# Attention sums of four batches kept in one bank per key head, and new values of four batches added together

## The chip, the core and the metric

The kernel runs on one core of a Trainium2 chip. Time is the device time of one execution in microseconds (us). Before the change the median of three runs was 2500.81 us (2497.43 to 2500.87).

The engines are named as in the profile: PE is the tensor engine (PEld its weight loads), DVE the vector engine, ACT the scalar engine, POOL the GpSimd engine, SP the engine that only issues DMA transfers. DMA transfers run on queues of their own. The tensor engine writes only to PSUM, a memory of eight banks, each of 512 float32 values in each of 128 partitions; the other data lie in SBUF.

## The reference

Four residual layers follow each other. Only the third, attention over a paged cache, is touched by the change.

```python
x = x + _L0_cond_ref(x, cond, w0)            # a 32x32 mix per batch
x = x + _L1_cond_ref(x, adapter, ...)        # linear layer and LoRA
x = x + _L2_cond_ref(x, Wq, Wk, Wv, Wo, ...) # attention
x = x + _L3_cond_ref(x, cond, w3)            # a 32x32 mix per batch

# _L2_cond_ref: 64 batches of 32 tokens, 32 query heads, 8 key heads, head size 128
q, k, v = x @ Wq.T, x @ Wk.T, x @ Wv.T       # then rms norm and rotary on q and k
kc = k_cache[block_table]                    # 16 pages of 32 keys per batch
vc = v_cache[block_table]
k_all = concatenate([kc, k], axis=1)         # 512 cached keys and 32 new ones
v_all = concatenate([vc, v], axis=1)
scores = einsum('bqhd,bkhd->bhqk', q, k_all) * SCALE
scores = where(valid, scores, -1e30)
o = einsum('bhqk,bkhd->bqhd', softmax(scores), v_all)
return o.reshape(bsz, seqlen, HQ * D) @ Wo.T
```

## The kernel before

The 2048 rows (64 batches of 32 tokens) make 16 tiles of 128 rows, that is of NB = 4 batches. The 8 key heads make NG = 2 groups of KG = 4. A step is one group and one tile, 32 in all; in the text below "a tile" of the attention is such a step. A step has four units, one for each batch, and a unit has four slots, one for each key head k of its group. So a step has 16 slots and the attention 512. A key head serves REP = 4 query heads, and 4 heads of 32 tokens give the 128 rows of one matmul.

The slots are a software pipeline written by hand. `slot(i)` (L1193) emits, in this order, what belongs to slot i: the scores of slot i (L838 and L841, two matmuls into the two banks of `s_ps`), the `flip` of slot i - 2 (L880: its probabilities are transposed, four blocks into the one bank of `pT_ps`, which VectorE copies to `pT`), pieces of the projection of later tiles (L651), and the `values` of slot i - 3 (L893: four matmuls over the cached values `v_sb`). Each engine executes what it is given in that order. Other work is put into slots by a plan, `at(slot, where, ...)`, and `run(i, where)` emits it at its place in the slot: "fetch" first, "act" and "store" last.

Three pieces of other work matter here.

New values. The 32 new keys of a unit have values too. The probabilities of the four key heads for them are transposed together (`flip_new`, L873) into `pT_new`, and `values_new` (L905) adds four matmuls with 32 rows each, one for each key head, at the end of each unit: 128 times.

Heads and pages. The projected queries and keys are normed and rotated by DVE, and four heads at a time are transposed on PE (`Norm.turn`, L756) and copied by ACT (`Norm.keep`, L768). During the first group's steps the key pages of the second group are turned likewise (`Turn.turn`, L272, and `Turn.keep`, L283).

Sums, copies and stores. Four banks of PSUM belong to the sums: three under the tag `o` for the key heads 0 to 2, and one, tag `o3`, for key head 3, which the heads and pages that are turned use as well. At the end of each unit `finish` copies the four sums to `oT` by two ACT copies (L919 and L922). At the end of a step, one slot later, `store` writes the whole `oT` (1 MB) to memory as one DMA (L929), on SP's queue, or on POOL's for the last three steps. The last layer reads it back later.

SP issues most transfers in order. In the "fetch" of every fourth slot it loads the keys of the next unit page by page: 16 DMAs (L794) into one of two buffers, after register loads from the page table. `fetch_new` (L816) loads `v_new`. `begin` (L825) puts a unit's new keys beside the cached ones. The cached values are gathered by POOL (L105).

The tile pools name their buffers: a tile with the same name goes round through `bufs` buffers, 2 by default in the pool `attn`, 1 in the PSUM pools. A new use waits until the last reader of that buffer is done, a DMA included.

Of the kernel before, what the change touches and what calls it, by code (L numbers as in the profile page):

```python
# [27 lines left out]
F32 = mybir.dt.float32  # L28
# [15 lines left out]
P = 128  # L44
B, S, HID = 64, 32, 512
NT = B * S // P
NB = P // S
NC = HID // P
D = 128
HK, REP = 8, 4  # L50
NPAIR = HK // 2
NG = 2
KG = HK // NG
# [24 lines left out]
def resid_kernel(  # L78
# [19 lines left out]
    nc = tc.nc  # L98
# [129 lines left out]
    with ExitStack() as l2:  # L228
# [11 lines left out]
        room = {}  # L240
# [8 lines left out]
        class Turn:  # L249
# [15 lines left out]

            def turn(self):
                if self.g:
                    self.ps = room["o"].tile([P, HID], F32, name="pageT_ps", tag="o3")
                else:
                    self.ps = ps_s.tile([P, 2 * HID], F32, name="s_ps")  # L270
                for k in range(KG):
                    nc.tensor.transpose(  # L272
                        self.ps[:, k * P : (k + 1) * P],
                        self.rows[:, k // 2, (k % 2) * D : (k % 2 + 1) * D],
                        ident,
                    )
# [10 lines left out]
            def store(self):  # L287
                c = self.c
                nc.sync.dma_start(
                    out=v_dram[self.g][c * P : (c + 1) * P, :].rearrange("k (i f) -> k i f", i=2),  # L290
                    in_=self.cached(1),
                )
                nc.sync.dma_start(
                    out=kT_dram[self.g][4 * c : 4 * c + 4].rearrange("p d f -> d p f"),
                    in_=self.turned.rearrange("d p k s -> d p (k s)"),
                )
# [400 lines left out]
        class Norm:  # L697
# [50 lines left out]
                nc.vector.tensor_tensor(self.a, self.a, self.b, ALU.add)  # L748

            def turn(self):  # L750
                if "o" in room:
                    self.tp = room["o"].tile([P, REP, P], F32, name="head_ps", tag="o3")
                else:
                    self.tp = ps_t.tile([P, REP, P], F32, name="head_ps", tag="t")
                for h in range(REP):
                    nc.tensor.transpose(self.tp[:, h, :], self.a[:, h, :], ident)  # L756

# [15 lines left out]
        class Unit:  # L773
# [38 lines left out]

            def fetch_new(self):

                self.v_new = room["v"].tile([P, D], F32, name="v_new", bufs=2)
                nc.sync.dma_start(  # L816
                    out=self.v_new,
                    in_=vn_dram[self.g][self.t][self.j * S : (self.j + 1) * S, :].rearrange(
                        "s (k d) -> k s d", k=KG
                    ),  # L820
                )

            def begin(self):

                nc.scalar.copy(  # L825
                    self.kT[:, NPP].rearrange("p k s -> p (k s)"),
                    step_of[self.s].kT_new[:, self.j].rearrange("p k s -> p (k s)"),
                )
                self.new = room["attn"].tile([P, KG, S], F32, name="p_new")
                self.sm, self.total, self.pT, self.o_ps = {}, {}, {}, {}  # L830

            def scores(self, k):

# [32 lines left out]
            def flip_new(self):  # L866


                if last_scores:
                    ps = last_scores.pop()[:, :P]  # L870
                else:
                    ps = ps_s.tile([P, 2 * HID], F32, name="s_ps")[:, :P]
                nc.tensor.transpose(ps, self.new.rearrange("p k s -> p (k s)"), ident)  # L873
                self.pT_new = room["attn"].tile([P, P], F32, name="pT_new", bufs=1)
                nc.scalar.copy(self.pT_new, ps)

            def flip(self, k):
# [6 lines left out]
            def values(self, k):  # L884


                if k == 0:
                    self.o_three = room["o"].tile([P, KG - 1, HID], F32, name="o_ps", tag="o")
                    self.o_ps = {i: self.o_three[:, i, :P] for i in range(KG - 1)}
                elif k == KG - 1:  # L890
                    self.o_ps[k] = room["o"].tile([P, HID], F32, name="o_ps3", tag="o3")[:, :P]
                for c in range(NC):
                    nc.tensor.matmul(  # L893
                        self.o_ps[k],
                        lhsT=self.v[c][:, k * D : (k + 1) * D],
                        rhs=self.pT[k][:, c, :],
                        start=(c == 0),
                        stop=False,
                    )

            def values_new(self):

                for k in range(KG):
                    rows_k = slice(k * S, (k + 1) * S)
                    nc.tensor.matmul(  # L905
                        self.o_ps[k],
                        lhsT=self.v_new[rows_k, :],
                        rhs=self.pT_new[rows_k, :],
                        start=False,
                        stop=True,  # L910
                    )

            def finish(self):
                if self.j == 0:
                    oT_of[self.s] = room["attn"].tile([P, KG * REP, P], F32, name="oT", bufs=1)
                dst = oT_of[self.s].rearrange("p (k h) s -> p k h s", k=KG)[
                    :, :, :, self.j * S : (self.j + 1) * S
                ]
                nc.scalar.copy(  # L919
                    dst[:, KG - 1], self.o_ps[KG - 1].rearrange("p (h s) -> p h s", h=REP)  # L920
                )
                nc.scalar.copy(  # L922
                    dst[:, : KG - 1],
                    self.o_three[:, :, :P].rearrange("p k (h s) -> p k h s", h=REP),
                )

            def store(self):
                queue = nc.sync if self.s < len(steps) - 3 else nc.gpsimd
                queue.dma_start(out=o_dram[self.g][self.t], in_=oT_of.pop(self.s))  # L929

# [4 lines left out]
        def at(slot, where, do, *args):  # L937
            plan.setdefault((slot, where), []).append((do, args))

        def run(slot, where):  # L940
            for do, args in plan.pop((slot, where), ()):
                do(*args)

        step_of, pair_of, unit_of, turn_of, first_of = {}, {}, {}, {}, {}
        oT_of, rot_of = {}, {}
        pieces = []
        busy = {}
        turning = set()
# [1 line left out]
        def norm_piece(slot):  # L950


            if not pieces or pieces[0][0] > slot or busy.get(slot, 0) >= 2 + (slot % 4 == 1):
                return
            busy[slot] = busy.get(slot, 0) + 1
            _, piece, norm = pieces.pop(0)
            piece()
            if norm:
                slot += 1
                while slot in turning or (slot - VLAG) % KG == KG - 1:  # L960
                    slot += 1
                turning.add(slot)
                at(slot, "turn", norm.turn)
                at(slot, "keep", norm.keep)
# [146 lines left out]
        for u in range(len(units)):  # L1111
            at(KG * (u - 1) if u > 1 else ready + 3 * u, "fetch", make, unit_of, u, Unit, u)
            at(KG * (u - 1) + 1 if u else -1, "pool", call, unit_of, u, "mask")
            for c in range(NC):
                at(KG * u - 1 + c, "pool", call, unit_of, u, "fetch_values")
            at(KG * u - 1, "fetch", call, unit_of, u, "fetch_new")
            at(KG * u - 2, "act", call, unit_of, u, "begin")


# [73 lines left out]
        def slot(i):  # L1193
            run(i, "fetch")
            run(i, "pool")
            new, k = None, i % KG
            if 0 <= i < n:
                new = unit_of[i // KG]
                new.scores(k)
            if LAG <= i < n + LAG:  # L1200
                turned = unit_of[(i - LAG) // KG]
                turned.flip((i - LAG) % KG)
            run(i, "pe")
            run(i, "late")
            run(i, "power")
            norm_piece(i)
            if LAG <= i < n + LAG and (i - LAG) % KG == KG - 1:
                turned.flip_new()
            run(i, "turn")
            if i >= VLAG:  # L1210
                old = unit_of[(i - VLAG) // KG]
                old.values((i - VLAG) % KG)
                if (i - VLAG) % KG == KG - 1:
                    old.values_new()
                    at(i, "act", old.finish)
                    if old.j == NB - 1:
                        at(i + 1, "store", old.store)
            if new:
                new.divide(k)
            run(i, "dve")  # L1220
            norm_piece(i)
            norm_piece(i)
            run(i, "keep")
            run(i, "act")
            run(i, "store")

# [269 lines left out]
```

## Time and profile before

| | |
|---|---|
| median of three runs | 2500.81 us |
| the profiled execution | 2498.24 us |
| its span, first to last instruction | 2496.5 us |
| mean granted clock of PE | 0.997 |
| PE, share of the span | 98% |
| DMA q1 (issued by SP), share of 16 engines' span | 38.0% |

The attention's slots run from about 220 us to 2112 us, together with the projections; the first 220 us are the first two layers, and after 2112 us PE multiplies by the output weights. The costliest lines that the change touches, from the profile's groups (busy time in us, then mean length of one in ns, then the idle time ahead of it and what ended it):

```profile
L893 PE MATMUL o_ps<-pT,v_sb 128*128 128x128 f32 x4096 | 541.2, 275 | 2.4 <-DMA v_sb<-v,v_rows 2.4
L905 PE MATMUL o_ps<-pT_new,v_new 32*128 32x128 f32 x1024 | 64.4, 321 | 0.0
L756 PE MATMUL head_ps<-ident,rot_a 128*128 128x128 f32 x640 | 96.1, 273 | 0.2 <-ACT oT L919 0.2
L768 ACT COPY qT<-head_ps 128x512 f32<-128x512 f32 x128 | 72.2, 564 | 2.9 <-PE head_ps L756 2.9
L919 ACT COPY oT<-o_ps 128x128 f32<-128x128 f32 x128 | 32.7, 255 | 9.9 <-PE o_ps L905 9.9
L922 ACT COPY oT<-o_ps 128x384 f32<-128x384 f32 x128 | 61.5, 480 | 0.0
```

A float32 matmul stands twice in the records (two passes), a transpose once. The ends of matmuls are modelled and overlap with the next, so the rate is read from start to start.

### The profile page before, as it was taken

How to read it: one execution, taken by the hardware profiler on the slowest of the kernel's cores; microseconds unless marked ns; L12 is line 12 of the kernel's file. 1: busy time of each engine (PE TensorE's matmuls, PEld its weight loads, DVE VectorE, ACT ScalarE, POOL GpSimd, SP SyncE). 2: the span in 40 equal slices, each digit the busy share in tenths (PEclk: the TensorE clock that was granted, in tenths of full speed). 3: DMA queues.
4: the chain of work that ended last, by engine and by line, in shares of the span. 5: the costliest groups of instructions: out<-in, count | busy, mean ns of one | idle time of the engine just before them, and what ended most of it. 6: DMA issues, size and time to landing. Idle time of an engine off the chain costs nothing.

```text
span 2496.5 us, 47363 instructions
## 1 busy us (share of the span) xinstructions
PE 2445.1 (98%) x13760; PEld 1857.8 (74%) x13760; DVE 1609.0 (64%) x3602; ACT 1398.9 (56%) x4135; POOL 1163.0 (47%) x1096
## 2 busy tenths in 40 slices
PE   7799999999999999999999999999999999999999
PEld 4455777777777777777777777777777788888887
DVE  5657777767777677777776777777777766433222
ACT  2225777777767676767777777777777765000000
POOL 4335655555555555655555555655555663000000
PEclk9999999999999999999999999999999999999999
DMA  7775666666666667766565656666657784333221
GB/s 244 237 218 182 190 196 192 203 184 201 184 201 185 200 193 239 242 188 194 178 199 173 188 176 189 176 186 176 193 169 220 247 267 149 115 128 127 86 85 60
DMA packets 448546, 459.19 MB, mean 184 GB/s; under 512 B 51425, under 2 KB 379489, under 8 KB 440481
## 3 DMA queue, kind: packets, MB, share of 16 engines
q1 hardware_dynamic: 398384, 291.24, 38.0%
q0 software_dynamic: 49904, 164.93, 21.6%
q8 instruction: 112, 1.84, 0.3%
q14 instruction: 146, 1.19, 0.2%
HBM read 384.66 MB, written 79.69 MB: 186 GB/s over the span
## 4 chain that ended last, share of the span: by engine, by line
PE 92%; DMA 2%; DVE 2%; issue 2%; SPq 1%; POOL 1%; ACT 0%; DVEq 0%; POOLq 0%; ACTq 0%
PE proj_ps L651 22%; PE o_ps L893 17%; PE out_ps L1320 15%; PE s_ps L838 10%; PE s_ps L841 8%; PE pT_ps L880 8%; PE head_ps L756 3%; PE l_ps L490 2%; PE o_ps L905 2%; DMA kT<-kT 1%; DMA v_sb<-v,v_rows 1%; SPq L794 1%; PE s_ps L873 1%; PE h_ps L474 1%; PE mix_ps L1338 1%
## 5 line engine op out<-in xcount | busy, mean ns | idle before, releaser
L105 POOL DMA_INDIRECT v_sb<-v,v_rows x512 | 539.2, 1053 | 362.3 <-PE o_ps L893 252.9
L846 DVE CUSTOM_DVE_ANT_0 sm<-s_ps,pen 128x544 f32<-128x544 f32 x512 | 370.9, 724 | 462.4 <-PE s_ps L841 449.9
L893 PEld LDWEIGHTS o_ps<-pT,v_sb 128*128 128x128 f32 x4096 | 518.8, 192 | 133.6 <-issue 124.8
L857 ACT ACTIVATE sm<-sm,top 128x544 f32<-128x544 f32 x512 | 382.0, 746 | 342.8 <-DVE top L846 342.7
L893 PE MATMUL o_ps<-pT,v_sb 128*128 128x128 f32 x4096 | 541.2, 275 | 2.4 <-DMA v_sb<-v,v_rows 2.4
L863 ACT ACTIVATE sm<-sm,share 128x512 f32<-128x512 f32 x512 | 369.9, 722 | 170.3 <-DVE share L862 169.0
L882 DVE COPY pT<-pT_ps 128x512 f32<-128x512 f32 x512 | 351.1, 686 | 1.9 <-PE pT_ps L880 1.9
L838 PE MATMUL s_ps<-kT,qT 128*128 128x288 f32 x1024 | 347.0, 420 | 4.5 <-DMA kT<-kT 3.8
L880 PE MATMUL pT_ps<-ident,sm 128*128 128x128 f32 x2048 | 307.3, 273 | 0.0
L841 PE MATMUL s_ps<-kT,qT 128*128 128x256 f32 x1024 | 305.0, 380 | 1.9 <-issue 1.5
L880 PEld LDWEIGHTS pT_ps<-ident,sm 128*128 128x128 f32 x2048 | 255.8, 141 | 51.3
L809 POOL TENSOR_SCALAR pen<-key_f,seq_f 128x544 f32<-128x544 f32 x128 | 279.3, 2182 | 11.8 <-DMA kT<-kT 0.5
L712 POOL TENSOR_SCALAR ss<-ss 128x4 f32<-128x4 f32 x160 | 54.1, 338 | 448.0 <-ACT sq L707 447.6
L841 PEld LDWEIGHTS s_ps<-kT,qT 128*128 128x128 f32 x1024 | 194.2, 190 | 56.9 <-issue 3.4
L663 DVE TENSOR_TENSOR raw<-proj_ps,raw 128x512 f32<-128x512 f32 x332 | 223.5, 685 | 9.7 <-PE proj_ps L651 4.4
L707 ACT ACTIVATE sq<-raw 128x128 f32<-128x128 f32 x640 | 197.1, 308 | 29.7 <-DVE raw L663 14.5
L651 PE MATMUL proj_ps<-sum,x 128*128 128x512 f32 x380 | 189.7, 602 | 8.0 <-DVE raw L663 7.9
L1370 ACT COPY p<-out_ps 128x256 f32<-128x256 f32 x7 | 2.6, 372 | 333.1 <-PE out_ps L1320 333.1
L714 POOL TENSOR_TENSOR rstd<-ss,minus_half 128x4 f32<-128x4 f32 x160 | 183.0, 1144 | 13.3
L105 POOL DMA_INDIRECT mix_rows<-in_w,cond_rows x32 | 32.7, 1021 | 309.8 <-DVE mix_diag L171 300.0
L838 PEld LDWEIGHTS s_ps<-kT,qT 128*128 128x128 f32 x1024 | 154.7, 191 | 21.9 <-issue 4.8
L1320 PE MATMUL out_ps<-w,o_in 128*128 128x256 f32 x768 | 167.1, 379 | 0.0
(175 smaller groups left out, 3499.4 us busy)
## 6 DMA issues: line engine op xcount, KB each, us to landing
kT<-kT SPq DMA_DIRECT2D x2048, 64.0 KB
o<-oT SPq DMA_DIRECT2D x29, 1024.0 KB
o_in<-o SPq DMA_DIRECT2D x28, 1024.0 KB
page_rows<-in_kv_cache SPq DMA_DIRECT2D x32, 256.0 KB
v<-in_kv_cache SPq DMA_DIRECT2D x32, 256.0 KB
kT<-page_rows SPq DMA_DIRECT2D x32, 256.0 KB
vn<-raw SPq DMA_DIRECT2D x32, 256.0 KB
v_sb<-v,v_rows POOLq DMA_INDIRECT x512
```

What stands on the lines that cost most here:

```text
L105: nc.gpsimd.indirect_dma_start(out=dst, out_offset=None, in_=table, in_offset=bass.IndirectOffsetOnAxis(ap=index, axis=0),)
L651: nc.tensor.matmul(self.ps, lhsT=self.pair.x[x][:, c if x == "b" else half.start + c, :], rhs=blocks(self.b)[w][:, c, :], start=(c == 0), ...
L809: nc.gpsimd.tensor_scalar(self.pen, key_f, seq_f[:, self.b : self.b + 1], BIG, ALU.is_ge, ALU.mult)
L838: nc.tensor.matmul(ps[:, first:HID], lhsT=q, rhs=self.kT[:, :n1, k, :], start=True, stop=True)
L841: nc.tensor.matmul(ps[:, HID : first + LA], lhsT=q, rhs=self.kT[:, n1:, k, :], start=True, stop=True)
L846: nc.vector.tensor_tensor_reduce(out=sm, in0=ps[:, first : first + LA], in1=self.pen, scale=1.0, scalar=3e38, op0=ALU.add, op1=ALU.min, ac ...
L857: nc.scalar.activation(sm, sm, AF.Exp, bias=top, scale=-1.0, accum_out=total)
L863: nc.scalar.activation(sm[:, :L], sm[:, :L], AF.Copy, scale=share)
L880: nc.tensor.transpose(ps[:, c, :], self.sm[k][:, c * P : (c + 1) * P], ident)
L882: nc.vector.tensor_copy(pT, ps)
L893: nc.tensor.matmul(self.o_ps[k], lhsT=self.v[c][:, k * D : (k + 1) * D], rhs=self.pT[k][:, c, :], start=(c == 0), stop=False,)
L1320: nc.tensor.matmul(ps[:, :HALF], lhsT=o[:, i, :], rhs=w[i // REP][:, i % REP, :], start=(i == 0), stop=(i == KG * REP - 1),)
```

## The change

The sums of a step stay in PSUM until all four of its batches are done. Each key head has a bank of its own (tags `o0` to `o3`), 4 batches of 128 columns; the first matmul of the step begins the bank, the others add or write into it. The new values of all four units are added together at the step's end, so `pT_new` and `v_new` have four buffers each, and `v_new` is fetched at other slots. `finish` is now one ACT copy for each key head (for the last step every second on DVE), one in each of four slots, and `store` one DMA of 256 KB for each, one slot after its copy. `oT` holds one key head and has the pool's two buffers. Heads and pages are turned in the bank of the probabilities (tag `t` of `ps_t`), after the values in the slot; their copies now follow at once, ahead of `divide`, and a unit's last slot is open to turns too.

```diff
             def turn(self):
                 if self.g:
-                    self.ps = room["o"].tile([P, HID], F32, name="pageT_ps", tag="o3")
+                    self.ps = ps_t.tile([P, HID], F32, name="pageT_ps", tag="t")
...
             def turn(self):
-                if "o" in room:
-                    self.tp = room["o"].tile([P, REP, P], F32, name="head_ps", tag="o3")
-                else:
-                    self.tp = ps_t.tile([P, REP, P], F32, name="head_ps", tag="t")
+                self.tp = ps_t.tile([P, REP, P], F32, name="head_ps", tag="t")
...
-                self.v_new = room["v"].tile([P, D], F32, name="v_new", bufs=2)
+                self.v_new = room["v"].tile([P, D], F32, name="v_new", bufs=NB)
...
-                self.pT_new = room["attn"].tile([P, P], F32, name="pT_new", bufs=1)
+                self.pT_new = room["attn"].tile([P, P], F32, name="pT_new", bufs=NB)
...
             def values(self, k):
-                if k == 0:
-                    self.o_three = room["o"].tile([P, KG - 1, HID], F32, name="o_ps", tag="o")
-                    self.o_ps = {i: self.o_three[:, i, :P] for i in range(KG - 1)}
-                elif k == KG - 1:
-                    self.o_ps[k] = room["o"].tile([P, HID], F32, name="o_ps3", tag="o3")[:, :P]
+                if self.j == 0:
+                    o_of[self.s, k] = room["o"].tile([P, NB, P], F32, name="o_ps", tag=f"o{k}")
                 for c in range(NC):
                     nc.tensor.matmul(
-                        self.o_ps[k],
+                        o_of[self.s, k][:, self.j, :],
...
-                        start=(c == 0),
+                        start=(self.j == 0 and c == 0),
...
-            def finish(self):
-                if self.j == 0:
-                    oT_of[self.s] = room["attn"].tile([P, KG * REP, P], F32, name="oT", bufs=1)
...
+        def finish(s, k, copy):
+            o_ps = o_of.pop((s, k))
+            oT = oT_of[s, k] = room["attn"].tile([P, REP, P], F32, name="oT")
+            copy(
+                oT.rearrange("p h (j s) -> p h j s", j=NB),
+                o_ps.rearrange("p j (h s) -> p h j s", h=REP),
+            )
+
+        def store(s, k):
+            g, t = steps[s]
+            queue = nc.sync if s < len(steps) - 3 else nc.gpsimd
+            queue.dma_start(
+                out=o_dram[g][t][:, k * REP : (k + 1) * REP], in_=oT_of.pop((s, k))
+            )
...
-                while slot in turning or (slot - VLAG) % KG == KG - 1:
+                while slot in turning:
...
-            at(KG * u - 1, "fetch", call, unit_of, u, "fetch_new")
+            at(u // NB * SLOTS + 4 + 3 * (u % NB), "fetch", call, unit_of, u, "fetch_new")
...
-            run(i, "turn")
             if i >= VLAG:
                 old = unit_of[(i - VLAG) // KG]
                 old.values((i - VLAG) % KG)
-                if (i - VLAG) % KG == KG - 1:
-                    old.values_new()
-                    at(i, "act", old.finish)
-                    if old.j == NB - 1:
-                        at(i + 1, "store", old.store)
+                if (i - VLAG) % SLOTS == SLOTS - 1:
+                    for u in range(old.u - NB + 1, old.u + 1):
+                        unit_of[u].values_new()
+                    for c in range(KG):
+                        last = old.s == len(steps) - 1
+                        copy = nc.vector.tensor_copy if last and c % 2 else nc.scalar.copy
+                        at(i if last else i + c, "act", finish, old.s, c, copy)
+                        at(i + 1 if last else i + c + 1, "store", store, old.s, c)
+            run(i, "turn")
+            run(i, "keep")
             if new:
                 new.divide(k)
             run(i, "dve")
             norm_piece(i)
             norm_piece(i)
-            run(i, "keep")
             run(i, "act")
             run(i, "store")
```

## The prediction

> **What bounds the kernel now.** First the page: its busy times, the row of the tensor clock, and the chain that ended last.
>
> ```profile
> PE 2445.1 (98%) x13760; PEld 1857.8 (74%) x13760; DVE 1609.0 (64%) x3602; ACT 1398.9 (56%) x4135; POOL 1163.0 (47%) x1096
> ...
> PEclk9999999999999999999999999999999999999999
> ...
> PE 92%; DMA 2%; DVE 2%; issue 2%; SPq 1%; POOL 1%; ACT 0%; DVEq 0%; POOLq 0%; ACTq 0%
> ```
>
> TensorE holds 92% of the chain; what shortens its queue shortens the kernel, and what makes it wait lengthens it. Next the timeline of TensorE where a tile ends (start, length, line). Call e the slot in which a tile's last values are summed, here the one that began at 999.85; e+1 begins at 1003.49, e+4 at 1014.32.
>
> ```profile
> 1002.07 1.05 PE L893 MATMUL o_ps<-pT,v_sb 128*128 128x128 f32 x8
> 1003.05 0.50 PE L905 MATMUL o_ps<-pT_new,v_new 32*128 32x128 f32 x8
> 1003.49 0.75 PE L838 MATMUL s_ps<-kT,qT 128*128 128x288 f32 x2
> 1004.08 0.59 PE L841 MATMUL s_ps<-kT,qT 128*128 128x256 f32 x2
> ...
> 1006.24 1.06 PE L893 MATMUL o_ps<-pT,v_sb 128*128 128x128 f32 x8
> 1007.14 0.65 PE L838 MATMUL s_ps<-kT,qT 128*128 128x288 f32 x2
> 1007.62 0.60 PE L841 MATMUL s_ps<-kT,qT 128*128 128x256 f32 x2
> ...
> 1016.54 1.05 PE L893 MATMUL o_ps<-pT,v_sb 128*128 128x128 f32 x8
> ```
>
> Start to start, the values (L893) take 0.98 before an L905 group and 0.90 without one; L905 takes 0.44; L838 after it 0.59 instead of 0.48. A group of new values thus costs 0.08 + 0.44 + 0.11 = 0.63 us of TensorE. The last line is the first use of the fourth sum bank after the tile's end: 16.54 - 3.49 = 13.05 us after e+1 began (so at 27 of the first 31 tile ends).
>
> Third the timeline of SP's queue at the same place:
>
> ```profile
> 1003.62 0.60 SPq L816 DMA_DIRECT2D v_new<-vn  x1
> 1004.67 0.34 SPq L929 DMA_DIRECT2D o<-oT  x1
> 1005.84 10.87 SPq L794 DMA_DIRECT2D kT<-kT  x16
> 1016.80 0.38 SPq L586 DMA_DIRECT2D x_a<-xT  x1
> 1018.09 0.59 SPq L816 DMA_DIRECT2D v_new<-vn  x1
> 1019.76 9.44 SPq L794 DMA_DIRECT2D kT<-kT  x16
> ```
>
> The keys of one unit take SP 9.4 to 10.9 us of issuing, in one run that nothing overtakes. Last, a stall of TensorE early in the kernel:
>
> ```profile
> 133.40 1.02 PE L651 MATMUL proj_ps<-sum,x 128*128 128x512 f32 x2
> ...
> 138.50 3.63 PE L651 MATMUL proj_ps<-sum,x 128*128 128x512 f32 x4 [2.77 <-DVE raw L663]
> ```
>
> Four such matmuls take 1.88 at 1008.49 and 3.63 here: after 2.77 us of idleness the clock was halved (the clock records: 0.5 from 138.4 to 141.8). All four TensorE gaps of 2.77 to 5.1 us between 50 and 220 us were followed by 3.4 to 6.8 us at half clock; the ones of 1.5 to 2.4 us were not.
>
> **What the Trainium skill says.** "TensorEngine Tiling (Array Packing)", Key Properties: changing the tiling mode drains the array, and different row tiles run at once. The trace agrees: the records inside an L905 group start in fours, 7 ns apart, the second four 214 ns later, and the losses sit at the two edges. "TensorE: Matmul & The Clock Gate", What's actually happening: the clock is halved after an idle window of about 3.4 us; the trace's half-clock stretches are 3.4 us or twice that. "PSUM — Partial Sum Buffer", Engine vs sequencer instructions: ScalarE's and VectorE's queues are strictly first in, first out, so a copy that waits holds all behind it. [...]Here the 28 stores vn<-raw between 300 and 2000 us, 256 KB from on-chip memory like the new ones, landed 2.1 to 4.4 us (median 2.6) after their issue, by the trace's completion events.
>
> **Part 1: new values four units at a time.** Matmuls stay (1024 records of L905), but 32 groups replace 128. Of the 0.63 us, two rounds of four cost 2 x 0.112 = 0.22 if the next round's weights load behind the running one, as everywhere else in the trace (0.112 a matmul of 128 columns; in the group the second loads start 108 ns after the first), and 2 x 0.214 = 0.43 if rounds follow at the observed 214 ns. The rest, 0.41 or 0.20, is the two switches. 96 groups go: 96 x 0.41 = 39 us, or 96 x 0.20 = 19 us. I take 39: 214 ns contains the first load, which nothing hides.
>
> **Part 2: heads and pages turned in the bank of the probabilities, after the values.** The turn now waits for DVE's copy of pT, and the next slot's flip for ACT's copy of the turn. From a slot's start: pT is copied by 2.5 us (1001.62 + 0.69 - 999.85), the turn comes at 3.1 (scores 0.92, flip 0.44, one projection 0.86, values 0.89): no wait. The turn's last result lands at 3.71, ACT takes 0.56 (L768), so the bank is free at 4.36; the flip's weight load would go at 4.25, but has 0.11 of hiding under the scores' last matmul. Nothing is lost if ACT is idle then; it is, its exp ends near 2.9 and the share now queues behind the copy, with two slots to spare. DVE is early (447 of 512 reductions L846 waited for TensorE). Bounds 0 and 0.15 us on 169 turns; I take 0.03: 5 us. If ACT ran late, each turn would show it. Turns may now stand in a unit's last slot too, which changes their places, not their number (153 with heads, 16 with pages, before and after, within the slots).
>
> **Part 3: sums, copies and stores by key head.** That a bank is begun once is a flag of its first matmul, no time. Four 512-wide copies a tile (about 0.56 each, as L768) replace eight (0.25 + 0.47 a unit, L919 and L922): ACT gains, off the path. oT shrinks to a quarter in two buffers. Copies stand in slots e to e+3, stores one slot later, four of 256 KB. For the first 29 tiles these go through SP, and that moves the second store past a run of keys: slot e+2's fetch, 16 loads, stands ahead of the store of slot e+2. The fourth copy (slot e+3) reuses the second copy's buffer, so it waits until that store has landed. Behind it on ACT wait the exps; and the fourth sum bank has one buffer, so the next tile's first values of that head, in slot e+4, wait for it on TensorE.
>
> From the start of e+1: first copy done about 0.6, its store 0.7 to 1.0, v_new 1.1 to 1.7 (it now stands in front of these keys), table loads 0.8 as between 1005.01 and 1005.84, keys from 2.5. The run takes 9.9 (median of the runs that no 1 MB store precedes; range 9.4 to 10.7): 12.4. Second store 12.5 to 12.85, landed 15.45. Copy 15.5 to 16.06; the bank's values at 16.2, with 0.05 for the semaphore and 0.11 for a weight load. They were due at 13.05, and slots e+1 to e+4 stay as long as before. Stall: 3.2 us a tile, between 2.2 (run 9.4, landing 2.1) and 5.8 (10.7 and 4.4).
>
> Two things follow. In every other tile four squares (0.43 each) stand between the copy and the next exp, so VectorE's takes come late and a projection waits about 0.7 once more: 0.35 a tile. And a gap of 3.2 us should halve the clock in about two of three tiles (by where it lies in the 3.4 us window; over about 2/3 of a window idle did it above), at about 1.5 us: 1.0 a tile. Sum 3.2 + 0.35 + 1.0 = 4.55; 29 x 4.55 = 132 us.
>
> The last three tiles store through POOL, where no run of keys stands; the last tile takes turns with VectorE: 1 us. New-value fetches come later but land two slots before use; four copies of pT_new remove a wait that was not seen. Nothing.
>
> **The sum.** -39 + 5 + 132 + 1 = +99 on the profiled execution's 2498.2 us (span 2496.5 and 1.7 around it): 2597. That execution lies 2.6 below the median 2500.8; I leave it at 2597.
>
> **Rivals.**
> - The stall without the clock: 29 x 3.55 = 103; 103 - 39 + 6 = +70: 2568. For it: the slots around are dense and the gap hardly fills a window. Against: 2.77 us sufficed once.
> - The switches alone: the store lands under the slots, and only parts 1 and 2 show: 2498 - 39 + 5 = 2464. It decides if the stall stays under 34 / 29 = 1.2 us a tile: the store landing 2.0 us earlier than I place it. For it: SP's waits in before are short; against: even 9.4 and 2.1 leave 2.2.
> - Rounds at 214 ns: the gain is 19, 2617; or every store landing late, 29 x (5.8 + 0.7 + 1.7) = 238, some 2700.
> - That the change does not do what it says: fewer groups and four banks are in the code; no chance given.
>
> **How the numbers follow.** Stall with clock losses 0.62, stall without 0.22, switches alone 0.10, worse 0.06. The time is the likeliest's, 2597. The range 2535 to 2670 holds the first two but for their ends: below by run, landing and no clock loss (29 x 2.2 = 64, -39 + 6, some 2530), above by the slower landing; faster and worse stay outside. Slower by over 0.2% (5 us, what can be told from no change here) 0.88, within 0.02, faster 0.10.
>
> **What would show it.** Right: 32 groups of L905's successor of 32 records, about 1.1 us long; TensorE idle some 3 us in each slot e+4, released by ACT's copy oT, which itself waited for the DMA o<-oT; SP issuing the second store right after 16 keys; half-clock stretches once a tile; the clock's mean below 0.99. Wrong: no waits on oT at the tile ends, or turns that wait for ACT in every slot.

## The result, and the profile after

| | before | after |
|---|---|---|
| median of four runs, us | 2500.84 | 2693.68 |
| lowest and highest | 2497.43, 2501.68 | 2685.67, 2698.57 |
| the profiled execution, us | 2498.24 | 2685.67 |
| its mean granted clock of PE | 0.997 | 0.979 |

The ratio is 1.0771, with a 95% interval of 1.0742 to 1.0800. The change costs 193 us; the forecast of 2597 us stood for 96 over the median of before. The direction and the main mechanism were right. The size was half of what came, and the time lies above the upper end of the range, 2670 us.

First the page of the changed kernel: its busy times, and the chain that ended last.

```profile
PE 2483.0 (93%) x13760; PEld 1871.2 (70%) x13760; DVE 1612.5 (60%) x3604; ACT 1387.8 (52%) x4005; POOL 1154.9 (43%) x1105
...
PE 73%; SPq 9%; DMA 6%; issue 5%; ACT 4%; DVE 2%; POOL 1%; ACTq 0%; DVEq 0%; POOLq 0%
PE proj_ps L651 17%; PE o_ps L887 14%; PE out_ps L1317 14%; PE s_ps L835 8%; SPq L791 8%; PE s_ps L838 6%; PE pT_ps L877 6%; DMA o<-oT 4%; PE head_ps L753 2%; PE l_ps L490 2%; SPq L783 1%; PE o_ps L900 1%; DMA v_sb<-v,v_rows 1%; ACT sm L860 1%; ACT oT L913 1%
```

TensorE had 92% of the chain and has 73%. In its place stand, above all, SP's issuing of keys (L791; SP had 1% before) and the landing of a store (o<-oT, 4%). Lines have moved up: the values are L887 (L893 before), the new values L900 (L905), the sum copies L913, the stores L921, the keys L791 (L794).

The groups that answer to those shown of before (busy us, mean ns, idle time ahead and what ended it):

```profile
L887 PE MATMUL o_ps<-pT,v_sb 128*128 128x128 f32 x4096 | 559.2, 280 | 109.3 <-ACT oT L913 101.0 <-DMA v_sb<-v,v_rows 5.4 <-issue 2.7
L900 PE MATMUL o_ps<-pT_new,v_new 32*128 32x128 f32 x1024 | 37.5, 283 | 0.0
L765 ACT COPY qT<-head_ps 128x512 f32<-128x512 f32 x128 | 75.0, 586 | 154.2 <-PE head_ps L753 116.7 <-issue 19.7 <-PE s_ps L838 11.3
L913 ACT COPY oT<-o_ps 128x512 f32<-128x512 f32 x126 | 72.4, 575 | 158.0 <-DMA o<-oT 124.4 <-PE s_ps L838 22.7 <-PE pT_ps L877 3.7
```

The new values got cheaper, as forecast. The values wait 101 us for the copies of the sums, which themselves wait 124 us for stores. And there is a wait that the prediction did not speak of: ACT's copies of turned heads (L765) now wait 117 us for the turn, against 2.9 before.

Two waits of TensorE in the changed kernel (us in total, times, longest):

```profile
PE o_ps L887 <- ACT oT L913: 101.0, 33, 6.8
PE proj_ps L651 <- ACT raw L671: 20.1, 27, 1.2
```

The second of them in the kernel before:

```profile
PE proj_ps L651 <- ACT raw L671: 1.2, 1, 1.2
```

Projections now wait for ACT 27 times and not once. VectorE waits longer for ACT as well (its shares 223 us, 66 before), but that alone is no loss: the faster kernel with three buffers and the take first (below) has 123 us of the same wait.

Now one tile's end. Timeline of TensorE in the changed kernel:

```profile
1012.94 1.17 PE L900 MATMUL o_ps<-pT_new,v_new 32*128 32x128 f32 x32
1014.04 0.75 PE L835 MATMUL s_ps<-kT,qT 128*128 128x288 f32 x2
...
1026.23 1.02 PE L651 MATMUL proj_ps<-wk,x 128*128 128x512 f32 x2
1030.43 1.16 PE L887 MATMUL o_ps<-pT,v_sb 128*128 128x128 f32 x8 [3.18 <-ACT oT L913]
```

The 32 records of the new values take 1.10 from start to start. Slot e+1 begins at 1014.04, and the first use of the fourth bank comes at 1030.43 after 3.18 us of idleness. SP's queue over the same time:

```profile
1014.75 0.33 SPq L921 DMA_DIRECT2D o<-oT  x1
1015.17 0.59 SPq L813 DMA_DIRECT2D v_new<-vn  x1
1017.53 9.76 SPq L791 DMA_DIRECT2D kT<-kT  x16
1027.40 3.32 SPq L921 DMA_DIRECT2D o<-oT  x3
```

The first store goes at once. The second is the first of the three that follow the 16 keys. ACT's queue:

```profile
1018.14 0.56 ACT L913 COPY oT<-o_ps 128x512 f32<-128x512 f32 x1
...
1029.80 0.59 ACT L913 COPY oT<-o_ps 128x512 f32<-128x512 f32 x1 [4.52 <-DMA o<-oT]
```

The second copy was done at 1018.70, its store was issued at 1027.40, and the fourth copy, which needs that buffer, started at 1029.80, some 2.0 us after that issue ended (1027.76). It is the chain that the prediction drew. Medians over the 28 tiles after the first, counted from the start of e+1: the keys begin at 3.3 us (forecast 2.5), the second store is issued at 13.5 (12.5), the fourth copy starts at 17.0 (15.5).

What such a stall leaves behind shows in the tile where it was longest (timeline of TensorE, then a view of stretches of the span: length, busy time of each engine, granted clock, DMA share, GB/s):

```profile
1099.41 2.08 PE L887 MATMUL o_ps<-pT,v_sb 128*128 128x128 f32 x8 [6.78 <-ACT oT L913]
1101.28 1.06 PE L753 MATMUL head_ps<-ident,rot_a 128*128 128x128 f32 x4
```

```profile
1090.30:1102.10 11.80, 5.02 (x24) 3.98 (x23) 3.52 (x7) 1.68 (x5) 3.74 (x4) 0.79 0.71 229
1102.10:1107.00 4.90, 4.90 (x22) 3.37 (x21) 2.58 (x6) 4.29 (x15) 1.24 (x2) 0.81 0.41 117
1107.00:1110.10 3.10, 3.10 (x20) 2.42 (x19) 2.00 (x6) 1.33 (x4) 2.59 (x4) 1.00 0.44 101
```

After the wait, eight records of values take 1.87 from start to start instead of 0.89, and the granted clock is 0.79 and 0.81 in two slots, then 1.00. The clock records have 20 stretches at half clock within the attention, 88.7 us together, and none there in the kernel before. At half speed that is at most 44 us lost, as far as TensorE is busy in them. Each begins in, or within 1.2 us after, one of the 29 gaps in slot e+4. The six of 6.8 us began 0.7 to 2.2 us before TensorE resumed, the 14 of 3.4 us at most 0.6 before it. Those 20 gaps lasted 2.4 to 6.8 us and the nine without a stretch 1.3 to 3.7, so the length of a gap alone does not decide.

### The profile page after: what moved, and what is told of

Read it like the earlier page. It is cut to its first block, busy times and chain, and to the rows that moved or that the text cites. A ratio compares the mean times of both kernels' runs of the same rounds, so it can differ in the third digit from the quotient of the medians.

```text
span 2683.7 us, 46987 instructions
## 1 busy us (share of the span) xinstructions
PE 2483.0 (93%) x13760; PEld 1871.2 (70%) x13760; DVE 1612.5 (60%) x3604; ACT 1387.8 (52%) x4005; POOL 1154.9 (43%) x1105
## 4 chain that ended last, share of the span: by engine, by line
PE 73%; SPq 9%; DMA 6%; issue 5%; ACT 4%; DVE 2%; POOL 1%; ACTq 0%; DVEq 0%; POOLq 0%
PE proj_ps L651 17%; PE o_ps L887 14%; PE out_ps L1317 14%; PE s_ps L835 8%; SPq L791 8%; PE s_ps L838 6%; PE pT_ps L877 6%; DMA o<-oT 4%; PE head_ps L753 2%; PE l_ps L490 2%; SPq L783 1%; PE o_ps L900 1%; DMA v_sb<-v,v_rows 1%; ACT sm L860 1%; ACT oT L913 1%
## 5 line engine op out<-in xcount | busy, mean ns | idle before, releaser
L887 PEld LDWEIGHTS o_ps<-pT,v_sb 128*128 128x128 f32 x4096 | 535.1, 195 | 315.9 <-issue 159.5
L887 PE MATMUL o_ps<-pT,v_sb 128*128 128x128 f32 x4096 | 559.2, 280 | 109.3 <-ACT oT L913 101.0
L877 PE MATMUL pT_ps<-ident,sm 128*128 128x128 f32 x2048 | 313.0, 276 | 4.1 <-issue 3.7
L838 PE MATMUL s_ps<-kT,qT 128*128 128x256 f32 x1024 | 310.7, 386 | 0.0
L877 PEld LDWEIGHTS pT_ps<-ident,sm 128*128 128x128 f32 x2048 | 250.6, 143 | 72.3 <-issue 17.0
L838 PEld LDWEIGHTS s_ps<-kT,qT 128*128 128x128 f32 x1024 | 199.0, 194 | 56.4
L859 DVE RECIPROCAL share<-total 128x1 f32<-128x1 f32 x512 | 81.8, 160 | 246.0 <-ACT sm L854 223.0
L714 POOL TENSOR_TENSOR rstd<-ss,minus_half 128x4 f32<-128x4 f32 x160 | 172.7, 1079 | 13.4
L835 PEld LDWEIGHTS s_ps<-kT,qT 128*128 128x128 f32 x1024 | 159.1, 196 | 17.1 <-DVE top L843 6.6
```

The lines of the kernel that those rows point to most:

```text
L835: nc.tensor.matmul(ps[:, first:HID], lhsT=q, rhs=self.kT[:, :n1, k, :], start=True, stop=True)
L838: nc.tensor.matmul(ps[:, HID : first + LA], lhsT=q, rhs=self.kT[:, n1:, k, :], start=True, stop=True)
L877: nc.tensor.transpose(ps[:, c, :], self.sm[k][:, c * P : (c + 1) * P], ident)
L887: nc.tensor.matmul(o_of[self.s, k][:, self.j, :], lhsT=self.v[c][:, k * D : (k + 1) * D], rhs=self.pT[k][:, c, :], start=(self.j == 0 and ...
```

## The experiments

Each run's time is a median; ratios are to the kernel before, measured beside it on the same chip (2500.8 for the changed kernel, 2497.5 to 2499.6 for the others). "ACT's take" is the copy of a block's first projection, explained with the run take first. The edits of e3 to e6 are made to the kernel with three buffers.

| run | oT buffers | stores | ACT's take | us | ratio, interval | clock |
|---|---|---|---|---|---|---|
| changed kernel | 2 | SP, a slot later | last | 2693.7 | 1.0771 (1.0742 to 1.0800) | 0.979 |
| e1_three_buffers | 3 | as changed | last | 2515.9 | 1.0061 (1.0043 to 1.0080) | 0.994 |
| e2_store_same_slot | 2 | SP, same slot | last | 2576.7 | 1.0312 (1.0294 to 1.0329) | 0.991 |
| e3_three_buffers_keep_late | 3 | as changed | last | 2506.8 | 1.0033 (1.0021 to 1.0044) | 0.996 |
| e4_three_buffers_per_unit | 3 | as changed | last | 2549.6 | 1.0200 (1.0183 to 1.0217) | 0.994 |
| e5_take_first | 3 | as changed | first | 2482.3 | 0.9932 (0.9919 to 0.9946) | 0.994 |
| e6_last_slot_closed | 3 | as changed | last | 2513.1 | 1.0066 (1.0051 to 1.0082) | 0.995 |
| e7_zeros_in_stall | 2 | as changed | last | 2630.3 | 1.0521 (1.0505 to 1.0537) | 0.994 |
| e8_two_buffers_take_first | 2 | as changed | first | 2630.5 | 1.0535 (1.0519 to 1.0551) | 0.978 |
| e9_pool_stores_take_first | 2 | POOL | first | 2481.9 | 0.9932 (0.9916 to 0.9949) | 0.994 |

### Three buffers

```diff
-            oT = oT_of[s, k] = room["attn"].tile([P, REP, P], F32, name="oT")
+            oT = oT_of[s, k] = room["attn"].tile([P, REP, P], F32, name="oT", bufs=3)
```

> The changed kernel, with three buffers for oT in place of two: a tile's fourth copy now takes the buffer of its first, whose store stands ahead of the keys on SP. Theory A (the wait of the fourth copy for the second store is nearly the whole loss, with the clock that it halves): the groups 'PE o_ps <- ACT oT' vanish, the mean granted clock is back at 0.99 or more, and the time is 2500.8 - 39 + 5 and what the projections' waits for ACT raw L671 cost (18.9 us in the trace): 2465 to 2490. Theory B (the copies of heads that now stand ahead of divide on ACT make the exps, shares and projections late, and the wait for oT only shows that lateness): stalls move to other lines and the time stays above 2550.

2515.9: 178 of the 193 us are gone with 2 KB more in each partition. The wait for the fourth bank is gone from TensorE's list, and the clock is back. Theory A holds for the ring of buffers. But the time is 26 us above the band that it gave, and still longer than before. The waits of TensorE in this run now begin with:

```profile
PE proj_ps L651 <- ACT raw L671: 30.4, 45, 1.2
```

### The store in its copy's slot

```diff
-                        at(i + 1 if last else i + c + 1, "store", store, old.s, c)
+                        at(i + 1 if last else i + c, "store", store, old.s, c)
```

> Two buffers as in the changed kernel, but each store is emitted in the slot of its copy and not one later, so that the second store stands ahead of the run of 16 key loads on SP and not behind it. Theory A: it is the place behind the keys that makes the store late; the waits on oT fall from 101 us to under 15, the time is within 15 us of the kernel with three buffers (a little above it, since SP waits for the copies with the keys behind it). Theory A2 (any ring of two is too short, since a store needs 2 to 4 us to land and the copies are one slot apart): the waits stay at half or more, 2560 to 2620. Theory B: no change, above 2650.

2576.7: no wait for a copy oT is left among TensorE's waits, so a second store ahead of the keys is early enough for two buffers. But the run is 61 us slower than three buffers, which no theory gave: the cost has moved. SP's queue at a tile's end in this run:

```profile
1086.60 0.32 SPq L921 DMA_DIRECT2D o<-oT  x1
1086.97 0.43 SPq L256 DMA_DIRECT2D page_rows<-in_kv_cache  x1
1091.66 0.33 SPq L921 DMA_DIRECT2D o<-oT  x1
1092.08 0.61 SPq L813 DMA_DIRECT2D v_new<-vn  x1
1093.79 9.64 SPq L791 DMA_DIRECT2D kT<-kT  x16
```

SP stands for 4.3 us before the second store, waiting for its copy, and the keys behind it begin 7.2 us after the first store instead of 2.8 above. Scores then wait for keys; among TensorE's waits:

```profile
PE s_ps L835 <- DMA kT<-kT: 14.8, 6, 3.9
...
PE s_ps L838 <- ACT sq L707: 8.7, 7, 2.0
PE s_ps L838 <- issue: 8.5, 4, 2.7
```

The last two name no transfer. I read them as late keys too, since only the stores were moved, and the keys with them; the trace does not show it. In every other tile the slot six after e lengthened from 3.97 to 5.98 and the one before it from 3.11 to 3.85 (means): 44 of the 50 us between the profiled executions of this run (2566.3) and of three buffers (2516.5).

### The copies of turned heads at their old place

```diff
             run(i, "turn")
-            run(i, "keep")
             if new:
                 new.divide(k)
             run(i, "dve")
             norm_piece(i)
             norm_piece(i)
+            run(i, "keep")
             run(i, "act")
```

> Three buffers, and the copies of turned heads stand on ACT where they stood in the kernel before, after divide and the pieces of the norm. Theory A says that what is left after the ring is a small loss from ACT's order: the waits 'PE proj_ps <- ACT raw L671' (18.9 us) go and the time falls by 10 to 20 us against three buffers alone; but the flip then waits for the late copy of the turn, in the bank of the probabilities, which could take back as much: between -20 and +15. Theory B: the order is the main loss, and this run is faster than three buffers alone by 50 or more.

2506.8, 9 less than three buffers alone: far from theory B's 50, and within the wider band of theory A. The projection's waits for ACT raw fell from 30.4 to 9.4, but weight loads of the flip (L877) waited 35.1 us for the copies instead of 19.1. With the turn in the bank of the probabilities, a copy that comes after divide frees that bank too late; put ahead of divide, it delays divide. Of the three slots named below, the wait is all but gone in two (0 and 11); the third (21), whose take stands behind a sum copy, stayed.

### New values at each unit's end again

```diff
-                if (i - VLAG) % SLOTS == SLOTS - 1:
-                    for u in range(old.u - NB + 1, old.u + 1):
-                        unit_of[u].values_new()
+                if (i - VLAG) % KG == KG - 1:
+                    old.values_new()
+                if (i - VLAG) % SLOTS == SLOTS - 1:
```

> Three buffers, and the new values are added again at the end of each unit (128 groups of 8 records in place of 32 of 32), into the same banks. This prices the fewer groups alone. If the switches cost 0.41 us each, as the prediction took, it is 96 x 0.41 = 39 us slower than three buffers alone (33 to 46); if rounds follow at 214 ns and only 0.20 was lost a group, 19 us (14 to 24).

33.7 us slower than three buffers alone (2549.6 to 2515.9). That is the price of 96 groups, 0.35 each. It lies at the lower edge of the band for 39 (33 to 46). The band for rounds at 214 ns with a loss of 0.20 a group (14 to 24) is excluded.

### The take of a block's first projection first

Where did the 50 us go between 2516 and 2466 (the time before, less 39 for the groups, plus 5 for the turns)? Apart from slots 2 and 18, in which tiles end and which now hold the 32 records of new values, three of the 32 slots of a pair of tiles had grown: 0, 11 and 21. (Means in us over 24 tiles, start of scores to start of scores; a slot's number is its place in the pair.)

| slot | before | changed | three buffers | take first |
|---|---|---|---|---|
| 0 | 3.11 | 4.50 | 4.00 | 3.11 |
| 11 | 4.61 | 5.18 | 5.15 | 4.07 |
| 21 | 3.59 | 4.43 | 4.43 | 3.59 |
| 6 (e+4) | 3.63 | 6.86 | 3.18 | 3.18 |
| 22 (e+4) | 3.63 | 8.51 | 3.57 | 3.57 |
| 2, 18 (e) | 4.49, 3.63 | 5.16, 4.44 | 5.16, 4.44 | 5.16, 4.44 |
| sum over 24 tiles | 1428 | 1581 | 1437 | 1405 |

All three come right after a block of projections began. Its first product is taken by ACT (L671), and the projections have one bank, so the next one waits for that take. The take stands at the end of its slot on ACT, behind all that the slot gave ACT. Timelines of ACT, then TensorE, with three buffers:

```profile
977.89 0.59 ACT L765 COPY kT_new<-head_ps 128x512 f32<-128x512 f32 x1 [0.91 <-PE head_ps L753]
978.37 0.73 ACT L860 ACTIVATE sm<-sm,share 128x512 f32<-128x512 f32 x1
979.00 0.31 ACT L861 ACTIVATE p_new<-sm,share 128x32 f32<-128x32 f32 x1
979.21 0.29 ACT L822 COPY kT<-kT_new 128x128 f32<-128x128 f32 x1
979.39 0.58 ACT L671 COPY raw<-proj_ps 128x512 f32<-128x512 f32 x1
```

```profile
975.50 1.02 PE L651 MATMUL proj_ps<-wq,x_a 128*128 128x512 f32 x2
...
980.03 1.55 PE L651 MATMUL proj_ps<-wq,x_a 128*128 128x512 f32 x3 [0.82 <-ACT raw L671]
```

The product was there at 976.5. ACT stood idle 0.91 us for the turn, with divide, a small copy and the take queued behind it. At the same place in the kernel before, no turn stood ahead of the take, and the slot was longer by a group of new values (timelines of before, ACT then TensorE):

```profile
972.04 0.72 ACT L863 ACTIVATE sm<-sm,share 128x512 f32<-128x512 f32 x1 [0.43 <-DVE share L862]
...
973.06 0.57 ACT L671 COPY raw<-proj_ps 128x512 f32<-128x512 f32 x1
```

```profile
971.97 0.50 PE L905 MATMUL o_ps<-pT_new,v_new 32*128 32x128 f32 x8
...
973.86 1.88 PE L651 MATMUL proj_ps<-wq,x_a 128*128 128x512 f32 x4
```

The take ended at 973.63 and the next projection began at 973.86. That is 0.23 us of room, less than the group took that the change removed from this slot: the group had been the cover. The edit:

```diff
-                at(last, "act" if i == 0 else "dve", block.take, i, norm)
+                at(last, "late" if i == 0 else "dve", block.take, i, norm)
```

("late" is emitted after the projections and ahead of the values, so the take goes ahead of the turn's copy, of divide and of the sum copies.)

> Three buffers, and ACT's take of a block's first projection (the copy raw, L671) is emitted before the turn and its copy instead of at the slot's end. Theory C (the 50 us by which three buffers alone miss 2466 is this take: it stands on ACT behind the copy of the turn, which now waits for the end of the slot, behind divide, or behind a tile's third sum copy, in three slots of each pair of tiles at about 0.9 us): the waits of a projection for ACT raw (29 us) go, the three slots lose 0.8 to 1.0 each, 16 x 2.75 = 44 us in all, and the time is 2516 - 44 = 2472 (2465 to 2480), faster than the kernel before. Theory D (turns in the bank of the probabilities hold up the flip, whichever order ACT has): the three slots stay long, 2500 to 2516.

2482.3, 34 us less than three buffers alone and 17 us less than the kernel before. The three slots are mended, as the table shows, and of the projections' waits for ACT raw one of 0.2 us is left. Theory C holds. It promised 44, of which 34 came: 2.8 a pair in most of the first fourteen pairs, but in the last two the run lost 3.9 us against three buffers alone, in slots where scores mostly waited for keys.

### The last slot closed to turns

```diff
-                while slot in turning:
+                while slot in turning or (slot - VLAG) % KG == KG - 1:
```

> Three buffers, and a unit's last slot is closed to turns again, as in the kernel before. In theory C one of the three slots (the eleventh of a pair of tiles, whose take stands behind a turn's copy that the kernel before did not have there) is mended and the two others are not: 16 us less than three buffers alone, about 2500 (2495 to 2508). In theory D turns only change places and the time stays at 2510 to 2520.

2513.1, not 2500: the intervals of this run and of three buffers overlap. The 0.5 us a pair that slots 10 and 11 gain is in part lost again where other turns moved (slot 23: 4.04 to 4.66). The wait in slot 11 fell from 0.82 to between 0.19 and 0.30 in 11 of 12 pairs and did not go, which agrees with the cover lost above. So the part of theory C that puts slot 11 down to the turn alone falls: about a third of its wait is there without one. It was 0.26 as well in the one pair of the run with three buffers where slot 10 had no turn.

### Zeros in the stall

In the changed kernel, twelve matmuls of zeros (`zero` is a tile set once) are added to the next tile's first sums in slot e+4, ahead of the values of the fourth head:

```diff
                 old = unit_of[(i - VLAG) // KG]
+                if (i - VLAG) % SLOTS == KG - 1 and 1 <= old.s < 30:
+                    for _ in range(12):
+                        nc.tensor.matmul(
+                            o_of[old.s, 0][:, 0, :],
+                            lhsT=ident,
+                            rhs=zero,
+                            start=False,
+                            stop=False,
+                            skip_group_check=True,
+                        )
                 old.values((i - VLAG) % KG)
```

> The changed kernel with its two buffers; in the slot in which TensorE waits for the fourth bank, ahead of the values, twelve matmuls more are issued that multiply zeros and add them to a bank already begun (12 x 0.224 = 2.7 us of 128x128x128, beside a wait of 3.1 to 3.7). If the stall's lower clock costs what the composition of the slots says (about 50 us over 29 tiles, matmuls after the wait running longer), TensorE now hardly idles there, the clock stays at 0.99, and in spite of 348 matmuls more the time falls by 30 to 50 us against the changed kernel: 2645 to 2665. If idleness does not cause the lower clock, or it costs nothing, the time stays within 10 us or rises (2685 to 2720).

2630.3: with 348 matmuls more the kernel is 63 us faster than the changed kernel. The zeros take 82.4 us, and 22.7 us of the wait for the fourth bank are left (line numbers are two higher here):

```profile
L1209 PE MATMUL o_ps<-zero,ident 128*128 128x128 f32 x696 | 82.4, 275 | 0.0
```

```profile
PE o_ps L889 <- ACT oT L915: 22.7, 24, 3.9
```

Together that is 105, so the stall itself is as long as in the changed kernel. What went is the lower clock (0.994, two stretches of 3.4 us in the attention instead of 20). Where the zeros filled the wait least, it shows again:

```profile
1068.27 2.84 PE L1209 MATMUL o_ps<-zero,ident 128*128 128x128 f32 x24
1074.96 1.79 PE L889 MATMUL o_ps<-pT,v_sb 128*128 128x128 f32 x8 [3.86 <-ACT oT L915]
1076.55 1.06 PE L755 MATMUL head_ps<-ident,rot_a 128*128 128x128 f32 x4
```

3.86 us idle, and the next eight values take 1.59 from start to start. The gain is above the band that was expected (30 to 50). Of 4.3 us a pair, 2.4 came in the slots in and after the gaps (6 to 8, 22 and 23); another 1.6 came in slots in which the clock was not low: slot 0 from 4.50 to 4.00, slot 3 from 3.90 to 3.28, slot 4 from 3.92 to 3.48. The low clock is not shown to be the cause of those.

### Two buffers, take first

The edit of the take alone, in the changed kernel.

> The changed kernel with its two buffers, and only the take of a block's first projection put ahead of the turn on ACT. If the two losses are separate and add up, it is 44 us faster than the changed kernel, about 2650 (2640 to 2660). If an earlier end of those slots only makes the fourth bank's wait longer, since the store behind the keys sets that time, the gain is half or less: 2670 to 2690.

2630.5, 63 us less than the changed kernel: more than the 34 that the same edit brings with three buffers, so the two losses do not simply add. Again slots 3 and 4 are back at 3.28 and 3.48, and the clock is not (0.978, 21 stretches at half clock), so the low clock alone does not lengthen them.

What lengthens slots 3 and 4 (e+1 and e+2 of every other tile) in the changed kernel is in part visible. There the first copy of the sums starts late in 12 of 15 such tiles, 1.4 to 2.9 us after e+1 began, and with the take first it starts at 0.1 in all 15. ACT, changed kernel, where e+1 began at 620.08:

```profile
621.55 0.59 ACT L913 COPY oT<-o_ps 128x512 f32<-128x512 f32 x1 [2.27 <-PE s_ps L838]
```

ACT stood idle ahead of this copy, as in all twelve (2.2 to 3.7 us), so it was not behind with its own work; and by TensorE's records the sums were done at 620.15. What it waited for is open. Engines tell each other by signals that something is done, and this trace is odd in its signals: 36 stretches of 1.0 to 2.1 us in the attention show none of any engine or transfer, 28 of them in slots 0 and 3, and for 594 of the 3115 instructions of TensorE that signal no signal is recorded at their end. The other traces have 0 to 11 such stretches, and 4 to 25 such instructions. Whether signals came late on the chip or went missing in the recording is not known, and the releasers named in this one trace are less certain for it.

### Two buffers, stores through POOL, take first

The edit of the take, and:

```diff
-            queue = nc.sync if s < len(steps) - 3 else nc.gpsimd
+            queue = nc.gpsimd
```

> Two buffers for oT as in the changed kernel and the take ahead of the turn, and all stores of sums go through POOL, where no run of key loads stands ahead of them and no copy holds up the keys. If the store's place behind the keys is what makes two buffers too few, the wait for the fourth bank goes (104 us in the twin whose stores go through SP, 2630) and the time is that of three buffers with the take first, 2482, plus what POOL loses: its stores wait for the copies with the gathers of values behind them, which had 0 to 12 us of slack: 2478 to 2500. If a ring of two is too short wherever the store stands, or the gathers come late as the keys did in the run with the store in the copy's slot, 2530 to 2620.

2481.9, the time of three buffers with the take first, with two. ACT's copies still wait for a store in three places:

```profile
ACT oT L913 <- DMA o<-oT: 5.6, 3, 3.1
```

Two buffers are enough; it was the store's place behind the keys that made them too few. On POOL the stores wait for the copies (81.7 us in the list of waits) with the gathers of values behind them, without a cost that shows in the time.

## Why the prediction was half right

The 194 us over the kernel before in the later sets (2499.2), from differences of runs (the intervals of the ratios leave some 4 us of uncertainty in each). The losses do not simply add, so the split between the first two lines depends on the order; this one takes the stall with the take already first. With the take last the stall is worth 178 us (2693.7 - 2515.9) and the take 34.

| term | forecast | measured | from |
|---|---|---|---|
| stall for the fourth bank, with its clock and what follows | +132 | +148 | two against three buffers, take first in both (2630.5 - 2482.3) |
| take of the first projection late | 0 | +63 (+34 without the stall) | take last against first with two buffers (2693.7 - 2630.5), with three (2515.9 - 2482.3) |
| fewer groups of new values | -39 | -34 | per unit against four at once (2549.6 - 2515.9) |
| the rest: turns, the last tile | +6 | +17 | take first against before (2482.3 - 2499.2 = -17), less the -34 |
| sum | +99 | +194 | |

- The mechanism of part 3 was right in each link: two buffers, the fourth copy waiting for the second store, that store behind 16 keys, the fourth bank's values in slot e+4 waiting for the copy. The stall was forecast at 3.2 us in 29 tiles, 93 us; 98 us were measured in slots e+4, 3.4 each. That it came so near is partly luck: the bank's values started at 17.6 after e+1 began, not at 16.2, since the keys began 0.8 later than worked out; but they were also due later, at 14.0 and not at 13.05, since the slots ahead of them did not stay as long as before (slot 21, slots 3 and 4). The landing of the stores vn<-raw was read too narrowly: counted from the end of the issue to the last completion event it was 2.0 to 5.0 us; the median of 2.6, which the sum uses, stands.
- What the prediction named to look for came: 32 groups of 1.1 us, TensorE idle at the tile ends, the store right after 16 keys, a clock below 0.99; the half-clock stretches came at 20 of 29 tile ends. "Turns that wait for ACT" did not come. It was ACT that waited for turns, 117 us, and that wait alone costs nothing: with the take first and three buffers it is 121 us, in a kernel faster than before. What costs is what stands behind it on ACT.
- The clock was mis-sized: 1.0 us a tile, 29 us. The clock records give up to 44 (half of 88.7); filling the gap with zeros gave 63, of which the part in slots 0, 3 and 4 is not shown to be the clock's. Two thirds of the gaps did halve it (20 stretches in 29 tiles), as taken; but six of the stretches lasted 6.8 us and not 3.4, and 1.5 us for one was too little.
- The step that failed is in part 2: "Nothing is lost if ACT is idle then; it is, its exp ends near 2.9 and the share now queues behind the copy, with two slots to spare." The share has slots to spare. What queues behind the share has not: at the end of the same slot ACT takes a block's first projection, which the only projection bank waits for, and the kernel before did that with 0.23 us to spare. I followed the moved copy to divide and stopped there. The third sum copy, in slot e+2, does the same to slot 21; part 3 counted it as no cost ("ACT gains, off the path"). Part 2 put 5 us on the turns and nothing on this take, and the take measured 34 us alone and 63 beside the stall. Of the 95 us that the sum lacks, 63 are this take when the stall is counted without it; counted the other way round, 34 are the take and 46 the stall.
- Part 1 was nearly right: 39 taken, 34 measured; in the slots a group was worth 0.55 and not 0.63, and four together 1.22. Each further group so adds 0.22, the two rounds of 0.112 that were taken, and the remaining 0.33 is close to the 0.35 that a saved group was worth.
- The last tile cost more than 1 us: TensorE's first product of the output waits 5.4 us for the second of VectorE's two copies (0.8 for ACT's before). In the run take first, three sums of output weights, 3.5 us, stand between the two on VectorE's queue, and the wait is 5.1. Of the 17 us of the rest this is some 4; the remainder was not separated.

Why the take costs 63 us beside the stall and 34 without it stays open. With the take first, or with the gap filled, slots 3 and 4 lose nothing; the changed kernel's trace shows ACT idle ahead of the first copy there, and not why.

The reading of the queue agrees with what the prediction cited from the Trainium skill, "PSUM — Partial Sum Buffer", Engine vs sequencer instructions: everything behind a waiting instruction on ScalarE waits with it. The trace shows it twice, at the fourth copy (4.52 us) and at the copy of a turn (0.91 us with the take behind it).

## What to carry to other kernels

When a copy is moved ahead in a strict queue, follow everything behind it to the end of the stage, not only the next instruction, and look for the one whose consumer has a single buffer. How many buffers a ring needs depends on the queue that frees them: here one buffer more was worth 178 us, and with the take first, stores on a queue without a long run in front did as well with two (2481.9 against 2482.3). The work that an edit removes may be what hid another engine's lateness; the slot that gets shorter shows what was beneath.

## What was not expected of the hardware

A gap of 2.4 us or more on TensorE can cost more than its length: 348 matmuls of zeros, 82 us of work put into the gaps, made the kernel 63 us faster, and the granted clock stayed at 0.994 instead of 0.979. The 20 half-clock stretches account for up to 44 us of that; the rest is not explained.
